# Graph attention and a routed FFN in one kernel: the first block's preparation moved ahead of a branch

## The chip, the cores and the metric

The kernel runs on one core of a Trainium2 chip. The core has a matrix engine (TensorE, PE, with its weight loads shown apart as PEld), a vector engine (VectorE, DVE), an activation engine (ScalarE, ACT), a general engine (GpSimd, POOL), a queue engine (SyncE, SP) and 16 DMA engines. [...] The metric is the device time of one execution in microseconds (us); lower is better.

## The reference

N = 4096 tokens of 256 numbers. A graph attention layer with four heads of 64 (mask `adj`, 4096 x 4096), a residual projection, ELU and layer norm; then a mixture of eight experts, two for each token. Cut to what matters here:

```
xn = layernorm(x)                                  # 4096 x 256
h = einsum('nd,hdk->hnk', xn, W)                   # 4 heads of 64
s_col = einsum('hnk,hk->hn', h, a1); s_row = einsum('hnk,hk->hn', h, a2)
e = leaky_relu(s_row[:, :, None] + s_col[:, None, :], 0.2)
att = softmax(where(adj > 0, e, -9e15), axis=-1)
out = einsum('hij,hjk->hik', att, h)
y = elu(out) + (xn @ Wr + br)
x = x + gamma * (y - mean(y)) / sqrt(var(y) + 1e-5) + beta
x = x + moe(layernorm(x))                          # top 2 of 8 experts, gelu
```

`adj` comes transposed; everything is float32, the masks bfloat16.

## The kernel before, in words

Tokens go in blocks of 512 (B; 8 blocks, NB) and row blocks of 128 (j, 32 of them, NT). Four sweeps (a, NR) each own 1024 rows of the output (R, two halves of 512), and run j over all 4096 columns.

*The attention of one j.* exp(leaky_relu(row + col)) is a product of factors: the larger of a row part (`er`, spread over all partitions) and a column part (`eb`), times a column factor that is multiplied into h (`ha`) and into the ones of the denominators (`unit`). So one DVE instruction for each head, `weigh` (L1067), makes w = max(er, eb) * mask, and PE adds up `acc` (L648, w times ha) and `den` (L657, w times unit). The mask `am` is loaded as int32 by SP and made bfloat16 by two ACT instructions (`load_mask`, L1055, L1056). w has ten buffers, the mask and its load three each.

*What must come first.* `norm_block(b)` (L520) loads 512 tokens (L523), takes mean and variance (`moments`, L173, L174), the root (`rstd_of`, with a square root on ACT, L138), normalises (xn, L528), transposes on PE (L533) and copies to `xT` on ACT (L537). `project_block(b)` (L542) makes h and the scores in one product (ph, L554, with `wall`: W and the score weights beside it) and the residual (pr, L578), subtracts a bound of the scores, `limit`, from the column scores and adds it to the row scores (sc, L561, L564), makes ed = exp of the column scores (L568) and ha (L569), the residual with its bias (rb, L583), and the row factor `part` (L593, L594), which is transposed (pp), copied (sp) and stored to `parts` in DRAM (L602). `load_rows` (L607) reads it back, the same numbers to all partitions, as `er`. Three PSUM banks (`bank`) serve pt, ph, pr, pp and pb in turn.

*The branch.* If `limit` is too large for the factors (`flag`), a general path is taken that works with maxima; with these inputs it is not. The branch (L976, L981) comes after `norm_block(0)`, `norm_block(1)`, `turn_biases` and the score weights (L469 to L497). Each engine reads the flag for itself. Behind it, in the path taken: `project_block(0)`, `load_rows`, then the sweep a = 0. Block b + 2 is normalised at j = 4b, and block b + 1 projected. Row blocks 0 to 3 are attended first for half 0 alone; then block 1 is projected, its row parts are loaded, and they are attended for half 1. From j = 4 on w has its full width of 1024.

The order inside an engine is a scheduler's, from dependences and priorities in program order; `issue_after(x)` makes it place what follows behind x, and `queue` fixes PE's order of acc and den. After sweep 0 nothing changes but the queue that an er is loaded on and its buffer.

Of the kernel before, what the change touches and what calls it, by code (L numbers as in the profile page):

```python
# [17 lines left out]
P = 128  # L18
# [22 lines left out]
def gat_then_moe(  # L41
# [49 lines left out]
    make_identity(nc, ident)  # L91

# [6 lines left out]
    nc.scalar.dma_start(wg[:, :, :E], Wg.rearrange("(c p) e -> p c e", p=P))  # L99
    bgb = const.tile([P, E], F32)  # L100
    nc.scalar.dma_start(bgb, over_partitions(bg, E))

    def numbers(name, shape, pattern, base=0, step=0):
        t = const.tile(shape, F32, name=name)
        nc.gpsimd.iota(
            t, pattern=pattern, base=base, channel_multiplier=step,
            allow_small_or_imprecise_dtypes=True,
        )
        return t
# [8 lines left out]
    nc.vector.tensor_scalar(before, ahead, 0.0, None, op0=OP.is_gt)  # L118
# [7 lines left out]
    nc.vector.tensor_copy(token16, token[:, :2])  # L126
# [21 lines left out]
    def mean_rstd(src):  # L148

        mv = moments(src)  # L150
        return mv, rstd_of(mv[:, :, 1], TB)

    def root_of(var, n):

        v = small.tile([P, n], F32, tag="v", name="v")
        nc.vector.tensor_scalar(v, var, EPS, None, op0=OP.add)
# [9 lines left out]
        return r  # L166
# [59 lines left out]
    nc.gpsimd.dma_start(b1r, b1.rearrange("e (c p) -> (e c) p", p=P))  # L226
# [222 lines left out]
    with ExitStack() as layer:  # L449
# [7 lines left out]
        ab = ab.rearrange("p (s k) -> p s k", s=2)  # L457
        for c in range(DC):
            nc.scalar.dma_start(
                wall[:, c, :HK].rearrange("p (h k) -> p h k", h=H),  # L460
                W[:, ts(c, P), :].rearrange("h p k -> p h k"),
            )
        nc.scalar.dma_start(ab[:, 0], over_partitions(a1, HK))
        nc.scalar.dma_start(ab[:, 1], over_partitions(a2, HK))
        nc.scalar.dma_start(wr, Wr.rearrange("(c p) d -> p c d", p=P))
        nc.scalar.dma_start(brm, over_partitions(br, D))
        nc.scalar.dma_start(gam, over_partitions(gamma, D))
        nc.scalar.dma_start(bet, over_partitions(beta, D))
        for c in range(DC):  # L469
            pr = large("wa").rearrange("p t d -> p (t d)")[:, : 2 * HK]  # L470
            pr = pr.rearrange("p (s k) -> p s k", s=2)
            nc.vector.tensor_tensor(
                pr, wall[:, c : c + 1, :HK].to_broadcast([P, 2, HK]), ab, OP.mult
            )
            nc.vector.tensor_reduce(
                wall[:, c, HK:], pr.rearrange("p s (h k) -> p (s h) k", h=H), AX.X, OP.add
            )

        nc.vector.tensor_scalar(brm, brm, -1.0, None, op0=OP.add)


        sq = gat.tile([P, H], F32)
        nc.vector.tensor_tensor(sq, wall[:, 0, HK : HK + H], wall[:, 0, HK : HK + H], OP.mult)
        for c in range(1, DC):
            s2 = gat.tile([P, H], F32, name=f"s2{c}")
            nc.vector.tensor_tensor(
                s2, wall[:, c, HK : HK + H], wall[:, c, HK : HK + H], OP.mult
            )
            nc.vector.tensor_tensor(sq, sq, s2, OP.add)
        long = gat.tile([P, H], F32)  # L490
        nc.gpsimd.partition_all_reduce(long, sq, P, bass_isa.ReduceOp.add)
        limit = gat.tile([P, H], F32)
        nc.scalar.activation(limit, long, AF.Sqrt, scale=1.01 * D)
        wide = gat.tile([P, 1], F32)
        nc.vector.tensor_reduce(wide, limit, AX.X, OP.max)
        flag = gat.tile([P, 1], I32)
        nc.vector.tensor_scalar(flag, wide, 0.5 * SPREAD, None, op0=OP.is_gt)  # L497

# [21 lines left out]
        def norm_block(b):  # L520

            xb = loaded("xb")
            nc.sync.dma_start(xb, rows_of(x, b))  # L523
            mv, r = mean_rstd(xb)
            pt = [bank([P, B], f"pt{c}") for c in range(DC)]
            for t in range(TB):
                xn = fin.tile([P, D], F32, tag="xn", name="xn", bufs=2)
                nc.vector.tensor_scalar(  # L528
                    xn, xb[:, t, :], mv[:, t, 0:1], r[:, t : t + 1],
                    op0=OP.subtract, op1=OP.mult,  # L530
                )
# [10 lines left out]
        def project_block(b, apart):  # L542
# [52 lines left out]
            else:  # L595
                nc.vector.tensor_copy(eb[:, here, :], cols)
                nc.vector.tensor_copy(turn, rows)
            pp = bank([H * TB, P], "pp")
# [3 lines left out]
            nc.gpsimd.dma_start(  # L602
                parts[:, ts(b, B)].rearrange("h (t p) -> h t p", p=P),
                sp,
            )

        def load_rows(er, b, n):  # L607

            src = parts[:, b * B : (b + n) * B]
            nc.scalar.dma_start(  # L610
# [301 lines left out]
        def last_block(b, u, z, given):  # L912
# [30 lines left out]
            r = root_of(mv[:, :, 1], TB)  # L943
# [7 lines left out]
            r = root_of(mv[:, :, 1], TB)  # L951
# [20 lines left out]

        norm_block(0)
        norm_block(1)
        turn_biases()
# [5 lines left out]
        with tc.If(general > 0) as chosen:  # L981

            with tc.tile_pool(name="gen", bufs=2) as work:
# [8 lines left out]
                for b in range(NB):  # L992
                    mine = range(b * B, (b + 1) * B)
                    rows = work.tile(full, F32, tag="er", name="er", bufs=1)
                    load_rows(rows, b, 1)
                    top = work.tile(full, F32, tag="top", name="top", bufs=1)
                    nc.vector.memset(top, -BIG)
                    for j in range(NT):
                        if j % TB == 0:
                            at = load_adj(work, mine, j, TB, 2)  # L1000
                        off = work.tile([P, B], F32, tag="off", name="off")
                        nc.vector.tensor_scalar(
                            off, at[:, j % TB, :], 0.0, -BIG, op0=OP.is_le, op1=OP.mult
# [12 lines left out]
                    for j in range(NT):  # L1016
                        if j % TB == 0:
                            at = load_adj(work, mine, j, TB, 2)
                        off = work.tile([P, B], F32, tag="off", name="off")
                        nc.vector.tensor_scalar(  # L1020
                            off, at[:, j % TB, :], 0.0, -BIG, op0=OP.is_le, op1=OP.mult
# [16 lines left out]
                    if b % HB == HB - 1 and b + 1 < NB:  # L1038
                        for _ in finish_blocks(b // HB):
                            pass  # L1040
# [292 lines left out]
```

## Time and profile before

| what | us |
|---|---|
| median of 3 runs | 1368.03 |
| lowest and highest of them | 1365.36, 1369.53 |
| the profiled execution | 1365.72 |
| its span, first to last instruction | 1364.0 |
| PE busy (matmuls) | 1292.6 |
| DVE busy | 868.1 |
| ACT busy | 597.2 |
| POOL busy | 226.6 |
| mean granted PE clock | 0.992 |

The profile is of one execution. A page lists groups of instructions with their busy time, the mean of one, and what ended the idle time ahead of them; the chain of waits goes back from the last instruction to what released it at each step; a timeline lists instructions in order of time; a view by stretches gives each engine's busy time in a stretch. The time is mostly three stages: preparation and sweep 0 to about 290 us, sweeps 1 to 3 to about 850, the experts after that. An idle engine costs time only where the engine that bounds the stage waits for it.

### The profile page before, as it was taken

What the parts mean: (1) busy time and instruction counts of PE and PEld (TensorE: products, weight loads), DVE (VectorE), ACT (ScalarE), POOL (GpSimd) and SP (SyncE); (2) the same over time, 40 slices, a digit from 0 to 9 for tenths busy, and PEclk for the clock granted to TensorE, in tenths of its full rate; (3) what the DMA queues carried; (4) which work ended last, traced back from release to release, by engine and by line L of the source; (5) the groups of instructions that cost most, each with busy time, mean ns of one, the idle gap of its engine ahead of it and who ended that gap; (6) DMA issues with size and microseconds to landing.
All of it is one profiled execution on the core that took longest, in us unless ns stands there. A gap on an engine that the chain in (4) does not pass through costs nothing.

```text
span 1364.0 us, 19028 instructions
## 1 busy us (share of the span) xinstructions
PE 1292.6 (95%) x7049; PEld 682.9 (50%) x7049; DVE 868.1 (64%) x1782; ACT 597.2 (44%) x1059; POOL 226.6 (17%) x189
## 2 busy tenths in 40 slices
PE   2889999999999999999999999999999999999996
PEld 1433333322222222222222222887788877888885
DVE  4789977878999989899999998665111111111110
ACT  1743533345566366654566552542333332333231
POOL 1000000000030300214000211125322212122221
PEclk9899999999999999999999999999999999999998
DMA  4654343343445444453333431977765665767671
GB/s 118 195 159 154 126 108 93 109 147 100 124 124 136 151 131 124 119 144 124 96 107 105 127 109 56 348 232 233 238 185 161 190 188 135 206 174 203 192 199 24
DMA packets 110270, 204.49 MB, mean 150 GB/s; under 512 B 8992, under 2 KB 77600, under 8 KB 110160
## 3 DMA queue, kind: packets, MB, share of 16 engines
q1 hardware_dynamic: 85792, 161.24, 37.7%
q0 software_dynamic: 19264, 32.27, 10.7%
q10 hardware_dynamic: 5104, 9.58, 2.4%
q8 instruction: 60, 0.98, 0.3%
q14 instruction: 50, 0.41, 0.1%
HBM read 173.99 MB, written 29.08 MB: 149 GB/s over the span
## 4 chain that ended last, share of the span: by engine, by line
PE 71%; DVE 19%; issue 3%; DMA 3%; ACT 2%; another core or an unknown queue 0%; ACTq 0%; POOL 0%; DVEq 0%; SPq 0%; POOLq 0%
PE acc L648 21%; PE po L1227 17%; PE ph L1207 16%; DVE w L1067 14%; PE den L657 10%; PE pr L578 1%; PE ph L554 1%; DMA b2b<-in_L_ffn_b 1%; DMA er<-parts 1%; PE pt L1189 1%; DVE y L874 1%; PE ptx L689 1%; DVE y L868 1%; PE pt L533 1%; DVE y L860 1%
## 5 line engine op out<-in xcount | busy, mean ns | idle before, releaser
L1067 DVE SCALAR_TENSOR_TENSOR w<-er,eb,am 128x1024 f32<-128x1024 f32 (+1 forms) x528 | 634.2, 1245 | 58.3 <-PE den L657 49.9
L648 PE MATMUL acc<-w,ha 128*64 128x512 f32 x2048 | 467.1, 601 | 7.2 <-DVE w L1067 5.0
L648 PEld LDWEIGHTS acc<-w,ha 128*64 128x64 f32 x2048 | 137.4, 137 | 301.7 <-issue 280.1
L1055 ACT ACTIVATE am<-adj 128x1024 bf16<-128x1024 int32 x132 | 139.5, 1057 | 287.8 <-DVE w L1067 280.2
L657 PE MATMUL den<-w,unit 128*2 128x512 f32 x2048 | 240.9, 593 | 7.7 <-DVE w L1067 6.7
L1207 PE MATMUL ph<-xT,w 128*128 128x256 f32 (+1 forms) x1056 | 241.9, 386 | 4.5 <-issue 2.4
L1227 PE MATMUL po<-w,hT 128*128 128x256 f32 x1088 | 240.6, 379 | 2.8 <-ACT hT L1211 2.8
L1211 ACT ACTIVATE hT<-ph,bias 128x256 f32<-128x256 f32 (+1 forms) x264 | 122.6, 476 | 257.2 <-PE ph L1207 252.8
L1207 PEld LDWEIGHTS ph<-xT,w 128*128 128x128 f32 x1056 | 199.9, 190 | 40.4 <-issue 3.2
L1227 PEld LDWEIGHTS po<-w,hT 128*128 128x128 f32 x1088 | 204.1, 190 | 29.6 <-ACT hT L1211 3.2
L1234 POOL DMA_INDIRECT out<-o,ids x68 | 107.0, 1574 | 357.5 <-DVE o L1231 188.3
L1231 DVE SCALAR_TENSOR_TENSOR o<-po,share,b2s 128x256 f32<-128x256 f32 x68 | 32.7, 482 | 192.3 <-PE po L1227 182.0
L1056 ACT ACTIVATE am<-am 128x1024 bf16<-128x1024 bf16 x132 | 139.3, 1057 | 2.9
L657 PEld LDWEIGHTS den<-w,unit 128*2 128x2 f32 x2048 | 44.7, 84 | 178.7 <-issue 152.0
L801 POOL DMA_INDIRECT lists<-xe,at x64 | 85.0, 1327 | 242.6 <-issue 127.3
L1193 DVE COPY xT<-pt 128x256 f32<-128x256 f32 (+1 forms) x29 | 12.6, 433 | 167.1 <-PE pt L1189 125.5
L1222 ACT ACTIVATE b2s<-b2b,share 128x256 f32<-128x256 f32 x68 | 31.5, 501 | 50.5 <-DMA b2b<-in_L_ffn_b 32.3
L878 POOL DMA_DIRECT2D out<-y x6 | 4.8, 800 | 256.0 <-DVE y L874 169.1
L554 PE MATMUL ph<-wall,xT 128*128 128x264 f32 x128 | 37.6, 418 | 7.7 <-DVE on L749 6.6
L578 PE MATMUL pr<-wr,xT 128*128 128x256 f32 x128 | 35.3, 403 | 2.6 <-ACT unit L568 0.9
L533 PE MATMUL pt<-ident,xn 128*128 128x128 f32 x64 | 14.7, 345 | 19.4 <-DVE xn L528 19.1
L554 PEld LDWEIGHTS ph<-wall,xT 128*128 128x128 f32 x128 | 25.3, 207 | 14.2 <-issue 8.1
(287 smaller groups left out, 640.6 us busy)
## 6 DMA issues: line engine op xcount, KB each, us to landing
adj<-in_adj SPq DMA_DIRECT2D x132, 512.0 KB
w<-in_L_ffn_W SPq DMA_DIRECT2D x66, 1024.0 KB
er<-parts ACTq DMA_DIRECT2D x3, 2048.0 KB
b2b<-in_L_ffn_b SPq DMA_DIRECT2D x33, 128.0 KB
early<-lists SPq DMA_DIRECT2D x16, 260.0 KB
xb<-in_x SPq DMA_DIRECT2D x8, 512.0 KB
residual<-rb POOLq DMA_DIRECT2D x8, 512.0 KB
rb<-residual SPq DMA_DIRECT2D x8, 512.0 KB
```

What stands on the lines that cost most here:

```text
L554: nc.tensor.matmul(ph, xT[:, c, ts(t, P)], wall[:, c, :], start=(c == 0), stop=(c == DC - 1),)
L578: nc.tensor.matmul(pr[:, t % 2, :], xT[:, c, ts(t, P)], wr[:, c, :], start=(c == 0), stop=(c == DC - 1),)
L648: queue(nc.tensor.matmul(acc[half][h // 2][ts(h % 2, K), :], ha[:, j, ts(h, K)], w[half][h], start=(j == 0), stop=(j == NT - 1),))
L657: queue(nc.tensor.matmul(den[h * Q : h * Q + HB, :], unit[:, j, h, 1 - half : 1 - half + HB], w[half][h], start=(j == 0 and half == 0), st ...
L801: ins = nc.gpsimd.indirect_dma_start(lists, bass.IndirectOffsetOnAxis(ap=at[:, k, t : t + 1], axis=0), xe[:, t, :], None,).ins
L1055: nc.scalar.activation(am, at[:, 0], AF.Relu)
L1056: nc.scalar.activation(am, am, AF.Sign)
L1067: nc.vector.scalar_tensor_tensor(wh[:, here], er[:, h, here], eb[:, j, h : h + 1], am[:, here], op0=OP.max, op1=OP.mult,)
L1207: order_of(nc.tensor.matmul(ph, job["w1"][:, c, ts(f, P)], xT[:, c, :], start=(c == 0), stop=(c == DC - 1),))
L1211: nc.scalar.activation(hT[:, f, :], ph, AF.Gelu, bias=job["bias"][:, f : f + 1])
L1227: order_of(nc.tensor.matmul(po, hT[:, f, ts(k, CH)], w2[:, f, :], start=(f == 0), stop=(f == FC - 1)))
L1234: nc.gpsimd.indirect_dma_start(job["into"], bass.IndirectOffsetOnAxis(ap=ids[:, k : k + 1], axis=0), o, None, compute_op=OP.add,)
```

## The change

- The root no longer uses ACT's square root in `norm_block` and for `limit`: `root_of` makes it with a first guess from the bits and three Newton steps on DVE. The sum over partitions for `limit` goes from POOL to two matmuls.
- Block 0 is loaded as four tiles; its normalisation is done by ACT instead of DVE.
- `project_first` projects block 0 ahead of the branch into the four acc banks, without the residual; `residual_first` makes that behind the branch. Block 0's row parts are stored on ACT's queue and loaded on SP's, ahead of the branch. The first two masks are made ahead of it too.
- The loads of a1 and a2 lead ACT's queue; five small ones go to POOL. POOL makes the identity before its counting tiles. `turn_biases` goes behind the branch. An Exp at the start loads ACT's table.
- Block 1's row parts are stored on ACT's queue instead of POOL's and loaded on SP's instead of ACT's.
- The general path (not taken) works in smaller tiles, so that er0 has room.

```diff
@@ -145,15 +149,11 @@
         nc.vector.tensor_tensor(r, r, q, OP.mult)
         return r
...
-    def root_of(var, n):
+    def root_of(var, n, part=1.0):
         v = small.tile([P, n], F32, tag="v", name="v")
-        nc.vector.tensor_scalar(v, var, EPS, None, op0=OP.add)
+        nc.vector.tensor_scalar(v, var, part, EPS, op0=OP.mult, op1=OP.add)
         r = small.tile([P, n], F32, tag="r", name="r")
         nc.vector.tensor_scalar(
             r.bitcast(I32), v.bitcast(I32), -0.5, 1597463007.0, op0=OP.mult, op1=OP.add
@@ -163,7 +163,7 @@
...
-        return r
+        return r, v
     def moments(src):
@@ -455,47 +454,54 @@
         brm = gat.tile([P, D], F32)
         ab = large("ab").rearrange("p t d -> p (t d)")[:, : 2 * HK]
         ab = ab.rearrange("p (s k) -> p s k", s=2)
+        nc.scalar.dma_start(ab[:, 0], over_partitions(a1, HK))
+        nc.scalar.dma_start(ab[:, 1], over_partitions(a2, HK))
         for c in range(DC):
             nc.scalar.dma_start(
                 wall[:, c, :HK].rearrange("p (h k) -> p h k", h=H),
                 W[:, ts(c, P), :].rearrange("h p k -> p h k"),
             )
-        nc.scalar.dma_start(ab[:, 0], over_partitions(a1, HK))
-        nc.scalar.dma_start(ab[:, 1], over_partitions(a2, HK))
         nc.scalar.dma_start(wr, Wr.rearrange("(c p) d -> p c d", p=P))
         nc.scalar.dma_start(brm, over_partitions(br, D))
-        nc.scalar.dma_start(gam, over_partitions(gamma, D))
-        nc.scalar.dma_start(bet, over_partitions(beta, D))
...
-        nc.vector.tensor_scalar(brm, brm, -1.0, None, op0=OP.add)
-        sq = gat.tile([P, H], F32)
-        nc.vector.tensor_tensor(sq, wall[:, 0, HK : HK + H], wall[:, 0, HK : HK + H], OP.mult)
...
-        long = gat.tile([P, H], F32)
-        nc.gpsimd.partition_all_reduce(long, sq, P, bass_isa.ReduceOp.add)
+        def rest_of_loads():
+            nc.gpsimd.dma_start(wg[:, :, :E], Wg.rearrange("(c p) e -> p c e", p=P))
+            nc.gpsimd.dma_start(bgb, over_partitions(bg, E))
+            nc.gpsimd.dma_start(gam, over_partitions(gamma, D))
+            nc.gpsimd.dma_start(bet, over_partitions(beta, D))
+            nc.gpsimd.dma_start(b1r, b1.rearrange("e (c p) -> (e c) p", p=P))
+        all1f = gat.tile([P, P], F32)
+        nc.vector.memset(all1f, 1.0)
         limit = gat.tile([P, H], F32)
-        nc.scalar.activation(limit, long, AF.Sqrt, scale=1.01 * D)
-        wide = gat.tile([P, 1], F32)
-        nc.vector.tensor_reduce(wide, limit, AX.X, OP.max)
         flag = gat.tile([P, 1], I32)
-        nc.vector.tensor_scalar(flag, wide, 0.5 * SPREAD, None, op0=OP.is_gt)
+        def scores_weights():
+            for c in range(DC):
...
+            sq = gat.tile([P, DC, H], F32)
+            nc.vector.tensor_tensor(sq, wall[:, :, HK : HK + H], wall[:, :, HK : HK + H], OP.mult)
+            pl = bank([P, H], "plim")
+            for c in range(DC):
+                nc.tensor.matmul(pl, all1f, sq[:, c, :], start=(c == 0), stop=(c == DC - 1))
+            r, v = root_of(pl, H, 1.01 * D)
+            nc.vector.tensor_tensor(limit, v, r, OP.mult)
+            wide = gat.tile([P, 1], F32)
+            nc.vector.tensor_reduce(wide, limit, AX.X, OP.max)
+            nc.vector.tensor_scalar(flag, wide, 0.5 * SPREAD, None, op0=OP.is_gt)
+        er0 = gat.tile([P, H, R], F32)
         ha = gat.tile([P, NT, HK], F32)
@@ -520,15 +526,31 @@
         def norm_block(b):
             xb = loaded("xb")
-            nc.sync.dma_start(xb, rows_of(x, b))
-            mv, r = mean_rstd(xb)
+            if b == 0:
+                for t in range(TB):
+                    nc.sync.dma_start(xb[:, t, :], x[ts(t, P), :])
+            else:
+                nc.sync.dma_start(xb, rows_of(x, b))
+            mv = moments(xb)
+            r, _ = root_of(mv[:, :, 1], TB)
+            if b == 0:
+                off = sums_of("off")
+                step.append(nc.vector.scalar_tensor_tensor(
+                    off, mv[:, :, 0], -1.0, r, op0=OP.mult, op1=OP.mult
+                ).ins)
             pt = [bank([P, B], f"pt{c}") for c in range(DC)]
             for t in range(TB):
                 xn = fin.tile([P, D], F32, tag="xn", name="xn", bufs=2)
-                nc.vector.tensor_scalar(
-                    xn, xb[:, t, :], mv[:, t, 0:1], r[:, t : t + 1],
-                    op0=OP.subtract, op1=OP.mult,
-                )
+                if b == 0:
+                    nc.scalar.activation(
+                        xn, xb[:, t, :], AF.Identity, bias=off[:, t : t + 1],
+                        scale=r[:, t : t + 1],
+                    )
+                else:
+                    nc.vector.tensor_scalar(
+                        xn, xb[:, t, :], mv[:, t, 0:1], r[:, t : t + 1],
+                        op0=OP.subtract, op1=OP.mult,
+                    )
                 for c in range(DC):
                     nc.tensor.transpose(pt[c][:, ts(t, P)], xn[:, ts(c, P)], ident)
             xT = (first_large if b < 2 else large)("xT")
@@ -595,19 +617,71 @@
             else:
                 nc.vector.tensor_copy(eb[:, here, :], cols)
                 nc.vector.tensor_copy(turn, rows)
+            store_parts(b, part, nc.scalar if b == 1 else nc.gpsimd)
+        def project_first():
+            sc = small.tile([P, TB, 2 * H], F32, tag="sc", name="sc")
+            cols, rows = sc[:, :, :H], sc[:, :, H:]
+            phs = [acc[t // 2][t % 2][:, : HK + 2 * H] for t in range(TB)]
+            for t in range(TB):
+                for c in range(DC):
+                    nc.tensor.matmul(
+                        phs[t], turned[0][:, c, ts(t, P)], wall[:, c, :],
+                        start=(c == 0), stop=(c == DC - 1),
+                    )
+                nc.vector.tensor_tensor(rows[:, t], phs[t][:, HK + H :], limit, OP.add)
+                nc.vector.tensor_tensor(
+                    cols[:, t], phs[t][:, HK : HK + H], limit, OP.subtract
+                )
+            part = small.tile([P, H, TB], F32, tag="part", name="part")
+            nc.vector.tensor_scalar(
+                part.rearrange("p h t -> p t h"), rows, 0.0, None, op0=OP.max
+            )
+            nc.scalar.activation(part, part, AF.Exp, scale=SLOPE - 1.0)
+            stored = store_parts(0, part, nc.scalar)
+            ed = unit[:, :TB, :, 1]
+            nc.scalar.activation(ed, cols, AF.Exp, scale=SLOPE)
+            nc.scalar.activation(eb[:, :TB, :], cols, AF.Exp, scale=1.0 - SLOPE)
+            step.append(stored)
+            for t in range(TB):
+                ins = nc.vector.tensor_tensor(
+                    ha[:, t, :].rearrange("p (h k) -> p h k", h=H),
+                    phs[t][:, :HK].rearrange("p (h k) -> p h k", h=H),
+                    ed[:, t].unsqueeze(2).to_broadcast([P, H, K]), OP.mult,
+                ).ins
+            step.append(ins)
+        def residual_first():
+            rb = residuals("rb")
+            for t in range(0, TB, 2):
+                pr = bank([P, 2, D], "pr")
+                for k in range(2):
+                    for c in range(DC):
+                        nc.tensor.matmul(
+                            pr[:, k, :], turned[0][:, c, ts(t + k, P)], wr[:, c, :],
+                            start=(c == 0), stop=(c == DC - 1),
+                        )
+                nc.vector.tensor_tensor(
+                    rb[:, t : t + 2, :], pr, brm.unsqueeze(1).to_broadcast([P, 2, D]), OP.add
+                )
+            nc.gpsimd.dma_start(rows_of(residual, 0), rb)
+        def store_parts(b, part, queue_of):
             pp = bank([H * TB, P], "pp")
             nc.tensor.transpose(pp, part.rearrange("p h t -> p (h t)"), ident)
             sp = small.tile([H * TB, P], F32, tag="sp", name="sp")
             nc.scalar.copy(sp, pp)
-            nc.gpsimd.dma_start(
+            return queue_of.dma_start(
                 parts[:, ts(b, B)].rearrange("h (t p) -> h t p", p=P),
                 sp,
-            )
-        def load_rows(er, b, n):
+            ).ins
+        def load_rows(er, b, n, queue_of):
             src = parts[:, b * B : (b + n) * B]
-            nc.scalar.dma_start(
+            queue_of.dma_start(
                 er,
                 bass.AP(
                     tensor=src.tensor, offset=src.offset, ap=[[0, P], [N, H], [1, n * B]]
@@ -970,9 +1044,32 @@
             last[0] = None
             listed.clear()
+        def load_mask(a, j):
+            at = load_adj(gat, range(a * R, (a + 1) * R), j, 1, 3)
+            am = gat.tile([P, R], BF16, tag="am", name="am", bufs=3)
+            nc.scalar.activation(am, at[:, 0], AF.Relu)
+            nc.scalar.activation(am, am, AF.Sign)
+            return am
+        warm = gat.tile([P, 1], F32)
+        nc.scalar.activation(warm, tiny, AF.Exp)
+        step = []
         norm_block(0)
-        norm_block(1)
-        turn_biases()
+        with tc.issue_after(step[-1]):
+            scores_weights()
+        project_first()
+        with tc.issue_after(step[-1]):
+            norm_block(1)
+            made_of_numbers()
+            nc.vector.tensor_scalar(brm, brm, -1.0, None, op0=OP.add)
+        with tc.issue_after(step[-2]):
+            first_masks = [load_mask(0, j) for j in range(2)]
+        load_rows(er0[:, :, :B], 0, 1, nc.sync)
+        rest_of_loads()
         general = nc.values_load(
             flag[0:1, 0:1], min_val=0, max_val=1,
             skip_runtime_bounds_check_because="a comparison gives 0 or 1",
@@ -1047,17 +1144,6 @@
             with tc.tile_pool(name="sep", bufs=2) as work:
...
                 def weigh(er, am, j, halves):
                     here = slice(halves[0] * B, (halves[-1] + 1) * B)
@@ -1073,9 +1159,10 @@
                     return w
                 both = list(range(HB))
-                project_block(0, True)
-                er = rows_parts()
-                load_rows(er[:, :, :B], 0, 1)
+                residual_first()
+                turn_biases()
+                ers = [er0, work.tile([P, H, R], F32, tag="er", name="er", bufs=1)]
+                er = er0
                 pending = None
                 for a in range(NR):
                     later = None
@@ -1084,10 +1171,11 @@
                             norm_block(j // TB + 2)
                         if a == 0 and j < TB:
-                            attend(weigh(er, load_mask(a, j), j, [0]), j, [0])
+                            am = first_masks[j] if j < len(first_masks) else load_mask(a, j)
+                            attend(weigh(er, am, j, [0]), j, [0])
                             if j == TB - 1:
                                 project_block(1, True)
-                                load_rows(er[:, :, B:], 1, 1)
+                                load_rows(er[:, :, B:], 1, 1, nc.sync)
                                 for i in range(TB):
                                     attend(weigh(er, load_mask(a, i), i, [1]), i, [1])
                             continue
@@ -1101,8 +1189,8 @@
                         if a + 1 == NR and j == 29:
                             first_tile()
                         if j == 20 and a + 1 < NR:
-                            later = rows_parts()
-                            load_rows(later, (a + 1) * HB, HB)
+                            later = ers[(a + 1) % 2]
+                            load_rows(later, (a + 1) * HB, HB, nc.scalar)
                     if a == 0:
                         mean_of_h()
                     er = later
```

The counting tiles get `issue_after` of the last instruction of the identity; `made_of_numbers` holds the two DVE conversions of `ahead` and `token` (L118, L126), and `mean_of_h`, `finish_blocks` and what follows them are as before.

## The prediction

> **What bounds the kernel now.** I read the page first: its span, its engine rows, its chain.
>
> ```profile
> span 1364.0 us, 19028 instructions
> PE   2889999999999999999999999999999999999996
> PE 71%; DVE 19%; issue 3%; DMA 3%; ACT 2%; another core or an unknown queue 0%; ACTq 0%; POOL 0%; DVEq 0%; SPq 0%; POOLq 0%
> L1067 DVE SCALAR_TENSOR_TENSOR w<-er,eb,am 128x1024 f32<-128x1024 f32 (+1 forms) x528 | 634.2, 1245 | 58.3 <-PE den L657 49.9
> ```
>
> TensorE (PE) is full in nearly every slice but the first (a slice is 34 us), and VectorE (DVE) waits for it, not it for DVE. The change touches only the start, so next come the stretches of the start (columns: busy us and instructions of PE, weight loads, DVE, ACT, POOL; granted clock; DMA):
>
> ```profile
> 27.00:66.00 39.00, 32.69 (x133) 18.35 (x135) 25.81 (x88) 25.00 (x37) 1.87 (x3) 0.91 0.66 204
> 66.00:80.00 14.00, 10.54 (x49) 6.97 (x45) 7.56 (x32) 5.52 (x15) 1.12 (x2) 1.00 0.62 189
> 80.00:92.00 12.00, 10.44 (x56) 2.22 (x56) 12.00 (x21) 7.75 (x8) 0.43 (x1) 0.86 0.42 129
> 92.00:118.00 26.00, 26.00 (x157) 7.93 (x151) 26.00 (x28) 12.26 (x17) 0.95 (x2) 1.00 0.45 144
> ```
>
> From 92 us PE has no gap. So whatever shortens the way there is gained whole, if PE then has as much work behind it. What lies on that way is in the chain of waits (start, us, what):
>
> ```profile
> 5.05 5.56 DMA ab<-in_L_gnn_a
> ...
> 18.63 1.32 PE pt L533 x4
> ...
> 23.66 3.67 issue
> ...
> 30.93 2.08 PE pr L578 x4
> ...
> 45.08 8.56 DMA er<-parts
> ...
> 72.05 7.77 DMA er<-parts
> ...
> 82.64 1.98 PE acc L648 x4
> ```
>
> Two loads of er (row parts of block 0, then of block 1, spread over all partitions) hold up the first attention; 3.67 us is the branch, and matmuls begin cold. Last, the timeline: where block 1's part is made, and where PE waits for DVE later.
>
> ```profile
> 65.34 0.17 DVE L593 TENSOR_SCALAR part<-sc 128x16 f32<-128x16 f32 x1
> ...
> 113.77 3.65 PE L648 MATMUL acc<-w,ha 128*64 128x512 f32 x16
> ...
> 148.19 0.44 PE L533 MATMUL pt<-ident,xn 128*128 128x128 f32 x2 [0.89 <-DVE xn L528]
> 179.57 0.44 PE L533 MATMUL pt<-ident,xn 128*128 128x128 f32 x2 [0.88 <-DVE xn L528]
> 210.84 0.44 PE L533 MATMUL pt<-ident,xn 128*128 128x128 f32 x2 [0.88 <-DVE xn L528]
> ```
>
> [...] flag written at 22.92, first DVE instruction of the taken side at 27.32, of PE at 27.95, of SP at 27.80; so 4.4 to 5.0 us, per engine, from its last instruction ahead of the branch. [...] four records of L578 take 2.08 us at 30.93 and 0.86 in a full stretch.
>
> **The change, part by part.** Times are of the profiled execution.
>
> (a) Up to block 0's xT. The x loads of block 0 become four and lead SP; ab leads ACT's queue, and five small loads go to POOL, behind its iotas, where nobody waits for them before the branch. The square root, its table load and its two hops to ACT go; root_of is 11 small DVE operations, each dependent on the last, at 0.2 us (L140 to L145 start at 16.30, 16.50, 16.70, 16.89). With the last x tile at 6.3 us (first statistics before: 6.34) DVE has the statistics at 6.9 and the offset, 12 operations on, at 9.3. ACT now does the four xn (0.5 each, from L1222's mean). But the identity is complete only at 11.66 (POOL, 11.38 + 0.28), as before; so PE starts at 11.7 instead of 16.2, and at 0.7 us per cold tile, with two xn buffers, ends at 14.9; xT at 16.0 (before 19.6). DVE's score weights (1.47 + 2 x 0.67) fit beside; the limit follows two tiny matmuls and 12 small operations by 16.5, under cover of the next step. The all-reduce on POOL and the ACT root go at no gain.
>
> (b) Block 0's projection ahead of the branch: eight matmuls[...]: done at 22. Part, exp, transpose, copy: 2 us; store issued at 24 and landed about 2.2 later (before: 2.5, 3.5 and 1.8 from issue of the store to that of the load), er issued at 26.2 on SP ahead of SP's branch, 7.8 us for the load: row parts at 34.
>
> (c) DVE ahead of the branch: four ha (1.4), block 1's statistics (1.8), three conversions (0.8), root (2.4), four xn with a wait for PE's cold transposes (2.4): from 22.7 to 31.8. The branch comes 8.9 us later than before, DVE's first w at 36.2 (before 53.66), PE's first instruction at 37.6. er at 34 is not what ends last.
>
> (d) After the branch. In the changed kernel's instruction order DVE has six w first, then residual_first's rb, then the norms of blocks 2 and 3 with the other ten half-width w, then block 1's projection. Counted up to block 1's part: 16 w x 0.67, 12 statistics x 0.35, 12 aggregates x 0.1, 6 xn x 0.35, 3 ha x 0.34, 3 rb x 0.6, some 50 small: 26 us. (The same prices on the old order from 27.3 to 65.4 give 25; the trace has 25.2.) residual_first runs cold on PE in front of the first attention: 2.1 + 2.1 + 1.9 + 1.0, so its two rb make DVE wait 1.7 and 1.2; waits for block 1's ph and pr I put at 0.9. So block 1's part comes at 36.2 + 26 + 3.8 = 66.0. Before it came at 65.34. The 17 us by which the first w is earlier are gone, because work that stood before the first w then stands behind it now.
>
> (e) From that part on: no table load and no POOL queue in the way; exp, transpose and copy 0.9, store 2.2, er with an x load ahead of it in SP's ring 8.3: 77.4 (before 79.85). Gain so far 2.4.
>
> (f) To the point where PE has no gap. DVE then has 16 half-width w and 8.9 us of other work (97.0), then sixteen full w at 1.2 with 11 us between: 127.2. PE ends row block 7 some 5.4 us on, at 132.6; before at 117.4. But in its order it has by then 14 ph, 16 pr and 12 transposes more behind it: 14 x 0.445 + 16 x 0.43 + 12 x 0.185 + 0.2 = 15.5. So 117.1 against 117.4: a gain of 0.3.
>
> (g) Later. Norm work being done early, DVE has 3.6 us besides w for the next four row blocks where it had 6 to 9, so the waits shown at 148, 179 and 210 should go: 2.65. Table loads of ACT in this stretch (1.28 each) go at nothing: ACT is busy 47% of the 26 us from 92. root_of costs DVE about 1 us a block, inside its slack. Rest unchanged.
>
> Sum: 0.3 + 2.65, about 3 us off an execution of 1365.7. The median of the runs is 1368.0; the same off it gives 1365.
>
> **Unknown costs.** Waits of DVE in (d): 3.8 taken; none would be 0, and between 27.3 and 65.4 DVE idled 38.1 - 25.2 = 12.9. er in (e): 7.8 if the SP ring is empty, 10 if it shares with adj and x loads. The clock in (b) and (d): all warm saves 4, all cold costs 3. Branch: 4.4 as before; a later flag gives no reason for less. ha and transposes waiting on ACT's four mask operations (1.06 each, ahead of block 1's xT): 0 to 2.
>
> **The rivals.** *The early start pays.* If DVE waits for nobody in (d), the store takes 1.8 and the ring is empty, another 3.8 + 0.4 + 0.5 come, and 2 if PE warms early: 1358. For it: er's first load at 34 and idle DMA between 12 and 28 us. Against: cold PE in front of the attention. *DVE's order decides (slower).* Up to row block 7 each wait of DVE goes through one to one. If it idles as it did, 12.9 instead of 3.8, the sum is 3 - 9: 1374. It decides from where block 1's part is later than 69 us, and makes the kernel measurably slower beyond 73. For it: DVE and PE feed each other there by sc, exp, ha and three PSUM banks. Against: those hops stand between other DVE work now. *It doesn't do what it says*: er lands late because store and load share rings with x and adj loads, at 42 instead of 34; 6 us of wait, 1371.
>
> **How the numbers follow.** What a measurement here can tell from no change is about 0.3%, 4.1 us. Forecast (1365, own range 1361 to 1369) 0.55; early start pays 0.22; DVE's order 0.18; late er 0.05. Of the forecast two fifths are below 1364, so faster 0.22 + 0.22 = 0.44; same 0.32 + 0.02 = 0.34; slower 0.18 + 0.03 + 0.01 = 0.22. The range 1357 to 1374 takes in both rivals' centres.
>
> **What would show it.** Right: first transpose of block 0 at about 12 us, store at 24, first w at 36 and ended by the branch, not by er; block 1's part at 64 to 68; second er at 75 to 80; no wait of PE for xn after 130. Wrong: first w ended by er beyond 40; the part before 61 or after 70; PE with gaps beyond 135; a different time in stages after 300 us, where nothing was changed.

## The result, and the profile after

| | us, median | lowest, highest |
|---|---|---|
| before | 1367.63 | 1365.36, 1369.53 |
| after | 1566.55 | 1563.21, 1569.53 |

The ratio is 1.1455, with a 95% interval of 1.1425 to 1.1484: the change makes the kernel 199 us slower. One run of five_masks, a kernel of the experiments, took 2258.62 us at a granted clock of 0.558, where its other eleven had 0.982 to 0.990, and is left out of its median and ratio. The page of after: its span, how busy PE was in forty equal slices and the clock granted to it there (in tenths, 9 is 90% or more), and three groups of instructions (busy us, mean ns of one, idle us ahead of them and what ended it):

```profile
span 1567.9 us, 19068 instructions
PE   3899998778888778887887787879999999999997
PEclk8999999989999989999999999999999999999998
L1153 DVE SCALAR_TENSOR_TENSOR w<-er,eb,am 128x1024 f32<-128x1024 f32 (+1 forms) x528 | 627.0, 1247 | 196.8 <-ACT am L1052 190.4
L722 PE MATMUL acc<-w,ha 128*64 128x512 f32 x2048 | 492.6, 623 | 53.1 <-DVE w L1153 52.9
L731 PE MATMUL den<-w,unit 128*2 128x512 f32 x2048 | 268.4, 644 | 102.7 <-DVE w L1153 102.6
```

The slices of the preparation are as good as before. The loss lies where no line of the attention itself was edited: from the seventh slice (235 us) to the 27th, the end of the sweeps, PE is at 7 or 8 tenths. The direction of waiting has turned round. Before, DVE's w waited 58.3 us in all, 49.9 of them for PE's den; now w waits 190.4 us for the mask (`am`), and PE waits for w. The number of w instructions and their mean length are the same. One stretch inside sweeps 1 and 2, the same 300 us of the clock before and then after (columns: busy us and instructions of PE, weight loads, DVE, ACT, POOL; granted clock, DMA share, GB/s):

```profile
300.00:600.00 300.00, 291.35 (x1792) 82.15 (x1786) 281.48 (x428) 171.18 (x286) 43.34 (x32) 1.00 0.44 127
```

```profile
300.00:600.00 300.00, 237.74 (x1316) 61.15 (x1312) 213.03 (x302) 126.21 (x207) 28.49 (x20) 0.92 0.34 100
```

No engine is full after the change; PE, the busiest, works 237.74 of 300 us. That fits a ring, engines that wait for each other in turn, and the timelines show one. First after (start and length in us), then before at the same place:

```profile
428.13 3.67 DVE L1153 SCALAR_TENSOR_TENSOR w<-er,eb,am 128x1024 f32<-128x1024 f32 x3
431.88 1.06 ACT L1051 ACTIVATE am<-adj 128x1024 bf16<-128x1024 int32 x1 [5.45 <-issue]
432.96 1.06 ACT L1052 ACTIVATE am<-am 128x1024 bf16<-128x1024 bf16 x1
434.06 4.87 DVE L1153 SCALAR_TENSOR_TENSOR w<-er,eb,am 128x1024 f32<-128x1024 f32 x4 [0.84 <-ACT am L1052]
439.01 1.06 ACT L1051 ACTIVATE am<-adj 128x1024 bf16<-128x1024 int32 x1 [2.09 <-issue]
```

```profile
434.49 1.27 DVE L1067 SCALAR_TENSOR_TENSOR w<-er,eb,am 128x1024 f32<-128x1024 f32 x1
434.51 1.06 ACT L1055 ACTIVATE am<-adj 128x1024 bf16<-128x1024 int32 x1 [1.94 <-DVE w L1067]
435.60 1.06 ACT L1056 ACTIVATE am<-am 128x1024 bf16<-128x1024 bf16 x1
435.79 1.28 DVE L1067 SCALAR_TENSOR_TENSOR w<-er,eb,am 128x1024 f32<-128x1024 f32 x1
439.68 1.06 ACT L1055 ACTIVATE am<-adj 128x1024 bf16<-128x1024 int32 x1 [3.02 <-DVE w L1067]
```

After: four w end, only then the Relu of the next mask starts, then its Sign, then the next four w. From Relu to Relu it is 439.01 - 431.88 = 7.13 us: 4.87 of w, 2.12 of ACT, 0.14 of hand-overs, for one j (a column block, as the expectations below call it). PE needs 5.3 us for one j: in the profile of before it does acc and den of two from 162.99 to 173.56 us. The view puts the waits of these two Relus down to "issue", that is to nothing that it could see; what they wait for comes next. Before: Relu and Sign run beside the w, for a later mask, and Relu follows Relu after 5.17 us. The kernel asks for three mask buffers both before and after, but after behaves as if it had one.

The built programs say why. The memory addresses that the 132 masks were given, and how many masks each address got:

```
before   44  44  44
after     1   1  130
```

Two addresses went to the two masks made ahead of the branch and were never given again; 130 masks share the third. In the program of after each Relu of the sweeps accordingly waits for the Sign of the mask just before it as well as for DVE; in that of before it waits for DVE alone.

### The profile page after: what moved, and what is told of

Read it like the earlier page. It is cut to its first block, busy times and chain, and to the rows that moved or that the text cites. A ratio compares the mean times of both kernels' runs of the same rounds, so it can differ in the third digit from the quotient of the medians.

```text
span 1567.9 us, 19068 instructions
## 1 busy us (share of the span) xinstructions
PE 1353.6 (86%) x7053; PEld 683.9 (44%) x7053; DVE 894.9 (57%) x1830; ACT 580.2 (37%) x1039; POOL 225.0 (14%) x190
## 5 line engine op out<-in xcount | busy, mean ns | idle before, releaser
L1153 DVE SCALAR_TENSOR_TENSOR w<-er,eb,am 128x1024 f32<-128x1024 f32 (+1 forms) x528 | 627.0, 1247 | 196.8 <-ACT am L1052 190.4
L722 PE MATMUL acc<-w,ha 128*64 128x512 f32 x2048 | 492.6, 623 | 53.1 <-DVE w L1153 52.9
L731 PE MATMUL den<-w,unit 128*2 128x512 f32 x2048 | 268.4, 644 | 102.7 <-DVE w L1153 102.6
L731 PEld LDWEIGHTS den<-w,unit 128*2 128x2 f32 x2048 | 41.4, 86 | 288.8 <-issue 145.3
L576 PE MATMUL ph<-wall,xT 128*128 128x264 f32 x112 | 33.3, 416 | 5.0 <-DVE rb L605 5.0
L921 ACT ACTIVATE y<-ptr,z 128x64 f32<-128x64 f32 x96 | 21.9, 324 | 34.5 <-PE ptr L919 30.5
L600 PE MATMUL pr<-wr,xT 128*128 128x256 f32 x112 | 30.6, 391 | 1.1 <-ACT xT L559 1.1
L609 POOL DMA_DIRECT2D residual<-rb x7 | 5.5, 779 | 157.1 <-DVE rb L605 97.6
```

What stands on the lines that cost most here:

```text
L576: nc.tensor.matmul(ph, xT[:, c, ts(t, P)], wall[:, c, :], start=(c == 0), stop=(c == DC - 1),)
L722: queue(nc.tensor.matmul(acc[half][h // 2][ts(h % 2, K), :], ha[:, j, ts(h, K)], w[half][h], start=(j == 0), stop=(j == NT - 1),))
L731: queue(nc.tensor.matmul(den[h * Q : h * Q + HB, :], unit[:, j, h, 1 - half : 1 - half + HB], w[half][h], start=(j == 0 and half == 0), st ...
L1153: nc.vector.scalar_tensor_tensor(wh[:, here], er[:, h, here], eb[:, j, h : h + 1], am[:, here], op0=OP.max, op1=OP.mult,)
```

## The experiments

The theory: *held buffers*. A mask that is allocated ahead of the branch keeps its buffer until the branch is over. Rivals: the *pool* (`load_mask` now takes its tiles from a pool opened ahead of the branch), and the *row parts* (one buffer of er ahead of the branch and one behind, other queues). In the table, "given" counts the buffers that the kernel asks for under the masks' name `am`, "held" those that masks made ahead of the branch keep, and "free" those left for the masks of the sweeps. Each ratio is to the kernel before as it ran beside that kernel; its medians there were 1364.85 to 1367.63 us, so kernels that ran apart are compared by ratio.

| kernel | given, held, free | us | ratio to before | 95% interval |
|---|---|---|---|---|
| after | 3, 2, 1 | 1566.55 | 1.1455 | 1.1425 to 1.1484 |
| masks_inside | 3, 0, 3 | 1366.02 | 1.0007 | 0.9995 to 1.0019 |
| masks_in_er0 | 3, 0, 3 | 1362.59 | 0.9994 | 0.9984 to 1.0004 |
| before_one_mask | 1, 0, 1 | 1566.70 | 1.1480 | 1.1454 to 1.1505 |
| before_two_masks | 2, 0, 2 | 1360.30 | 0.9973 | 0.9961 to 0.9986 |
| one_early_mask | 3, 1, 2 | 1359.59 | 0.9941 | 0.9919 to 0.9963 |
| five_masks | 5, 2, 3 | 1369.88 | 1.0025 | 1.0014 to 1.0037 |
| one_step_mask | 3, 2, 1 | 1430.78 | 1.0465 | 1.0438 to 1.0491 |
| own_masks | 2, 0, 2 | 1359.17 | 0.9936 | 0.9919 to 0.9953 |
| masks_in_er0_two | 2, 0, 2 | 1361.12 | 0.9951 | 0.9934 to 0.9968 |
| four_xn | 2, 0, 2 | 1358.28 | 0.9932 | 0.9915 to 0.9949 |
| late_residual | 2, 0, 2 | 1360.90 | 0.9954 | 0.9940 to 0.9968 |
| own_mask_four_xn | 2, 0, 2 | 1356.54 | 0.9924 | 0.9911 to 0.9938 |

**What costs the 199 us.** The line that makes the first masks is moved behind the branch:

```diff
-        with tc.issue_after(step[-2]):
-            first_masks = [load_mask(0, j) for j in range(2)]
...
+                first_masks = [load_mask(0, j) for j in range(2)]
                 residual_first()
```

> The changed kernel with its first two masks made inside the branch instead of ahead of it; same pool, same tag, same three buffers, same addresses. Theory of the held buffers (the two masks made ahead of the branch keep two of the three buffers until the branch is over, so that 130 masks share one): 1360 to 1372 us, the relu of the next mask beside the w of this one. Rival, the pool (a mask in the pool opened ahead of the branch waits too strictly, wherever it is made): 1555 to 1575. Rival, the row parts' second buffer or its queue: 1555 to 1575 too.

1366.02: the whole loss is gone, with the same pool, three addresses of 44 masks each, and the row parts as the change has them. Pool and row parts fall. Next, the masks stay early but lie elsewhere:

```diff
...
-            first_masks = [load_mask(0, j) for j in range(2)]
+            first_masks = [load_mask(0, j, er0[:, j, B:].bitcast(BF16)) for j in range(2)]
```

> The changed kernel with its first two masks still made ahead of the branch, but written into the half of er0 that is empty until the second row block, so that none of the three mask buffers is held. Held buffers: 1357 to 1370 us, and if the early masks are worth anything, up to 5 us below the kernel with the masks made inside. Rival, that a mask made ahead of the branch itself is what holds the sweeps up: 1555 to 1575. Rival, the pool or the row parts' buffer: 1555 to 1575.

1362.59: making masks early is not what hurts, holding their buffers is. The two loads of `adj` are still made ahead of the branch here, so their buffers are not it either. Then the loss put into the kernel before, by `bufs=1` in place of 3 for `am`, and the step between, `bufs=2`:

> The kernel before with one mask buffer instead of three and nothing else changed. Held buffers: the whole loss comes with it, 1555 to 1580 us, with the relu waiting for the fourth w of each column block. Rivals (pool, row parts): little of the loss, 1365 to 1420.

> The kernel before with two mask buffers instead of three. Held buffers: with two, relu and sign of the next mask (2.1 us) run beside the four w (4.9 us), so most of the loss is gone: 1365 to 1385 us. If the wait grows in step with the number of buffers taken away: about 1465. Rivals: 1365 to 1370.

One buffer gives 1566.70, a ratio of 1.1480 where after has 1.1455, the same within their intervals. Its group of w answers to that of after:

```profile
L1067 DVE SCALAR_TENSOR_TENSOR w<-er,eb,am 128x1024 f32<-128x1024 f32 (+1 forms) x528 | 626.8, 1247 | 192.5 <-ACT am L1056 189.9
```

The same 190 us of waiting for the mask. Two buffers lose nothing and are even 0.27% faster than three. So the price is a step between two and one, not a slope; one early mask (`range(1)`) says the same of the change itself:

> The changed kernel with one mask made ahead of the branch instead of two, nothing else. Held buffers: one of three is held, the sweeps have two, and with two the kernel before lost nothing, so 1357 to 1366 us. Rival, that any mask made ahead of the branch holds the sweeps up, or that the loss grows by the held buffer: 1450 to 1480.

1359.59, within its range: with one early mask in place of two the change is 0.59% faster than before, by an interval that excludes no change. And `bufs=5`, for which one of the ten w buffers was given up:

> The changed kernel with five mask buffers instead of three, so that three are left beside the two held ones; the memory comes from one of the ten w buffers. Held buffers: 1357 to 1368 us although both early masks and the pool are untouched. Rival, that the early masks' place or the pool matters and not the count: 1550 to 1570.

1369.88, 2 us beyond the range, but the 199 us are gone with both early masks in place. At PE's first wait for xn after 140 us this kernel was 3.7 us ahead of before (144.52 against 148.19), at the first expert 4.9 behind (859.0 against 854.1). The nine w buffers are the edit that reaches the sweeps; I didn't try them alone, so why it lost 8.6 us there is open. Last, the ring itself, by leaving the Relu out of it:

```diff
-            nc.scalar.activation(am, at[:, 0], AF.Relu)
-            nc.scalar.activation(am, am, AF.Sign)
+            nc.scalar.activation(am, at[:, 0], AF.Sign)
```

> The changed kernel with the mask made by one ACT instruction (Sign alone) instead of two; the Relu, which clamps negative entries, is left out. Theory of the ring: with one free buffer a column block takes four w (4.87 us), Relu and Sign (1.06 each) and their hand-overs one after another, 7.1 us; without Relu 6.05, so 132 masks x 1.08 = about 142 us less, 1420 to 1440 us, still slower than before because PE needs less than 6 us. Rival, that ACT's time is not in the ring (the next mask waits for something else, such as the load of adj): 1550 to 1570.

1430.78, 136 us less where 142 were worked out: the Relu stands in the ring nearly one to one (1.03 us a mask for its 1.06).

**What the change is worth without its fault.** Early masks in buffers of their own:

```diff
-            am = gat.tile([P, R], BF16, tag="am", name="am", bufs=3)
...
+            if first:
+                am = gat.tile([P, B], BF16, tag="am0", name="am0", bufs=2)
+            else:
+                am = gat.tile([P, R], BF16, tag="am", name="am", bufs=2)
...
```

> The changed kernel with the two early masks in buffers of their own, half as wide (only their first 512 columns are read), and two buffers for the masks of the sweeps: as much memory as three masks. Held buffers: the loss goes. Row parts not held up as in the kernel with the masks in er0 (there their load was issued at 27.4 us, behind the mask writes, against 24.8 in the changed kernel): first w at 34 to 35 us, and what was 2.7 us ahead of before at the norm of 145 us becomes 4 to 6. Time 1354 to 1361 us, ratio 0.993 to 0.998. Rival, that a start earlier by 2 us is taken back in the row blocks 0 to 2: the same as the next kernel, 1357 to 1363.

> The kernel with the early masks in er0, and two buffers in place of three for the masks of the sweeps. Two mask buffers gave the kernel before 0.27%: if that adds to the early masks' gain, 1354 to 1361 us (ratio 0.992 to 0.998). If both are the same 3 us (the ACT order in the first row blocks), 1359 to 1363 (0.997 to 1.000).

> The kernel with the early masks in er0 and two mask buffers, and four xn buffers in place of two. My step (g) had said that the three waits of PE for xn go because the norms have less company on DVE; they stayed at 0.71, 0.88 and 0.88 us. If they come from the two xn buffers (the third xn is queued behind w on DVE until PE has turned the first), they go with four: 2.5 us less than the kernel with two xn buffers, no wait of PE for xn over 0.35 us after 130 us. Rival, that xn stands behind w on DVE whatever its buffers: the waits stay, no difference.

1359.17 is within its range. 1361.12 is 0.1 us beyond one range and within the other, but its ratio, 0.9951 (to 0.9968), lies in that of the first case alone, which speaks for two gains that add. four_xn, 1358.28, is 2.8 us below it; the two ran side by side, and all six runs of four_xn (1357.57 to 1359.46) are below all six of masks_in_er0_two (1359.66 to 1361.55), so this difference is clear though their intervals against before overlap. The timeline shows the first waits of PE for xn in own_masks, and what stands in their place in four_xn (`bufs=4` for xn on top of masks_in_er0_two):

```profile
143.23 0.76 PE L555 MATMUL pt<-ident,xn 128*128 128x128 f32 x4 [0.63 <-DVE xn L550]
173.80 0.44 PE L555 MATMUL pt<-ident,xn 128*128 128x128 f32 x2 [0.88 <-DVE xn L550]
```

```profile
145.22 1.13 PE L600 MATMUL pr<-wr,xT 128*128 128x256 f32 x4 [0.62 <-ACT xT L559]
179.04 1.13 PE L576 MATMUL ph<-wall,xT 128*128 128x264 f32 x4 [0.87 <-DVE sc L586]
```

own_masks is 5.0 us ahead of before at the first (148.19) and 5.8 at the second (179.57). With four xn buffers the waits for xn are gone; a wait for xT or sc, about as long, comes instead, and yet by the first wait of sweep 1 the kernel is 2.2 us ahead of its like with two (287.07 against 289.27). Fewer waits are the smaller part of that: for the same matmuls from 140 us on (to 218.9 with two buffers, to 216.7 with four) PE waited 2.4 us and then 1.9, but its 24 transposes, eight at a stretch instead of four or two, were busy 3.3 us instead of 4.5, and the 158 acc 36.3 instead of 37.2. So the 2.5 us that were expected came, but mostly not as waits saved, and that part was luck.

Then residual_first, moved from the start of the branch to just ahead of block 1's projection in own_masks:

> The kernel with the early masks in buffers of their own, and residual_first moved from the start of the branch to just ahead of block 1's projection. Step (d) had put 2.9 us of DVE waiting on its cold matmuls in front of the first attention. If they are paid there, block 1's part, at 60.4 us in the kernel with own masks, comes at 57.5 to 59.5, and the time falls by 1 to 2 us. Rival, that its work is only moved behind the first attention and into the way of block 1's projection: part at 60 to 62, same time.

The time, 1360.90, can't be told from that of own_masks (the intervals overlap), but the stage differs: block 1's part came at 66.49 us instead of 60.38, later than the rival had allowed. At the start of the branch, in own_masks, these matmuls run from 34.56 to 40.62 us, where DVE makes its first six w (33.80 to 37.87); put later, they stand between those of the attention and of block 1 (49.35 to 59.7 us), ahead of block 1's projection. That this is what delays the part is read from the timeline, not tested. And the best parts together, with one early mask:

> One early mask in a buffer of its own and half as wide, two buffers for the masks of the sweeps, four xn buffers. If the gains of own masks (4 us by 180 us against masks in er0) and of four xn (2.2 us between 145 and 287 us) add up: 1353 to 1358 us, ratio 0.990 to 0.993. If not: 1357 to 1360.

1356.54, 0.76% faster than before, with an interval that excludes no change. It is the fastest of all; that the two gains add up in full isn't shown, as its interval overlaps those of own_masks and four_xn.

## Why the prediction was wrong

It was 1365, and 1566.55 was measured. The step that failed is (g), in two words: "Rest unchanged." In its place the sweeps' w waited 190.4 us for their masks. The cost of the early masks was put down only in the unknowns, as ACT time ahead of block 1's xT, 0 to 2 us. That they *own* two of three buffers for the length of the branch was priced nowhere, and no rival had it. The prediction's signs of being wrong did name "a different time in stages after 300 us, where nothing was changed". But something was: `load_mask` had moved, and the description before the prediction is wrong where it calls the er's queue and buffer the only change after sweep 0. A buffer count was read as a supply, when it is a limit on what is alive at once. The ring could have been priced from the page of before: four w at 1.25, two mask operations at 1.06, 7.1 us for one j, against the 5.3 that PE needs.

Of the other steps, in the profile of after up to where the masks bite:

```profile
21.88 0.18 DVE L638 TENSOR_SCALAR part<-sc 128x16 f32<-128x16 f32 x1
22.98 1.19 ACTq L676 DMA_DIRECT2D parts<-sp  x1
24.84 0.38 SPq L684 DMA_DIRECT2D er<-parts  x1
34.50 2.08 DVE L1153 SCALAR_TENSOR_TENSOR w<-er,eb,am 128x512 f32<-128x512 f32 x3 [4.65 <-DMA er<-parts]
61.90 0.18 DVE L615 TENSOR_SCALAR part<-sc 128x16 f32<-128x16 f32 x1
74.25 2.08 DVE L1153 SCALAR_TENSOR_TENSOR w<-er,eb,am 128x512 f32<-128x512 f32 x3 [1.79 <-DMA er<-parts]
```

- (a), (b): the times nearly right. The first transposes came at 10.95 (11.7 forecast), but not for the identity's sake: POOL had it done at 1.76 us, not at 11.66 as before, and PE waited for ACT's xn. ACT's table load at the early Exp took 1.28 us, at 6.24. Block 0's eight matmuls, whose end at 22 was an estimate, ran from 15.39 to 21.64. The part began at 21.88, the store issued at 22.98 (24) and the load at 24.84 (26.2). From the load's issue to the first w it was 9.7 us, not 7.8.
- (c): the time nearly right, 34.50 against 36.2, the reason wrong: DVE was done with block 1's xn at 29.85, not 31.8, and er ended last by the profile, though the branch (4.4 us before) was over at nearly the same time. In own_masks, where the load was issued at 24.2, er did not end last: w began at 33.80, 4.60 us after DVE's last instruction ahead of the branch.
- (d): 61.90 against 66.0. The start was 1.7 earlier; between the two DVE was busy 24.9 (26 forecast) and idle 2.5 (3.8). The matmuls of residual_first were slow (its 16 records on PE have a median of 631 ns, the 112 of the later blocks one of 379), but the two waits for them were 1.5 together, not 2.9, and late_residual shows that its place is cover rather than cost.
- (e): 74.25 against 77.4. The earlier part gave 4.1 us; the way from it took 12.4, not 11.4: from the load's issue, at 64.78 behind an x load at 64.34, to the first w it was 9.5 us, where the 8.3 of the forecast was an estimate.
- (f): 0.3 us was too little. With free buffers the change is 2.7 (masks_in_er0) or 5.0 (own_masks) ahead at 145 us. Most of that came from the earlier steps: at the second er own_masks was 6.7 ahead (73.17 against 79.85), where 2.4 were forecast, and on the way to 145 us it lost 1.7, where 2.1 were forecast. I had counted that way on the changed kernel's own order of instructions, in which w comes four at a time with everything else between (74.25, 79.21, 84.49 and 89.73 us): the order that held buffers make. In own_masks the order is before's kind again, and from the second er to block 3's part it takes 46.4 us (to 119.59), before 45.5 (to 125.30).
- (g): the three waits for xn were to go for lack of other norm work on DVE. They stayed in own_masks, at 0.63, 0.88 and 0.88 us, and went with four buffers, though others came in their place: with two, the third xn stands behind w on DVE until PE has turned the first (in before it began at 147.73 us, as four w begun at 142.94 ended).

So the 3 us of the sum were made of two errors, too little up to (f) and too much in (g). That masks_in_er0 is 2.7 us ahead at 145 us is therefore no proof of the sum; its time, 0.06% below before, can't be told from no change. Of the 0.64% of own_masks some 0.27% may be what two buffers give the kernel before as well.

Two of the prediction's readings of the branch before were off: SP's first instruction behind it is at 27.37 us, not 27.80, and the 5.0 us of PE run from the flag; from PE's last instruction ahead of the branch it was 6.59.

The loss adds up. The span grew by 203.9. PE was not busy for 214.3 us after and 71.4 before, 142.9 more; the other 61.0 are longer matmuls (1353.6 busy against 1292.6, with the same work), den 644 ns for 593, acc 623 for 601.

## What to carry to other kernels

Before moving an allocation ahead of a branch or loop, count what stays alive across it: a tile made outside and read inside took its buffer out of rotation, and the instructions that then wait are far from the edit. The built program shows it without a run, in the addresses given to the tiles of one name and in a wait of each producer for the one before. A stage with no full engine may be a ring: add up its members' durations once around (here 7.13 us), and compare that with what the bounding engine needs (5.3).

## What the runs showed of the hardware

PE was granted less than its full clock where its waits were short. In after the longest wait of PE between 300 and 420 us was 2.84 us, and in nine of the 24 stretches of 5 us there the granted clock was under full, 0.50 to 0.94; over 300 to 600 us it was 0.92, before 1.00. The wait of 2.84 us came after 13 us of matmuls without one, and half clock followed; after one of 2.51 us the clock stayed full (first lines from the timeline, second ones from the view by stretches: PE's busy us and instructions, granted clock, DMA share, GB/s):

```profile
334.63 1.97 PE L722 MATMUL acc<-w,ha 128*64 128x512 f32 x4 [2.84 <-DVE w L1153]
335.00:340.00 5.00, 4.58 (x12) 0.50 0.15 33
```

```profile
360.27 1.90 PE L731 MATMUL den<-w,unit 128*2 128x512 f32 x16 [2.51 <-DVE w L1153]
360.00:365.00 5.00, 4.73 (x30) 1.00 0.93 197
```

That the waits cost the clock, and how long one has to be for it, these runs don't show. The ends of matmuls are modelled in the profile, so the length of such a wait is not exact.

Two mask buffers in place of three took 0.9973 of before's time. With three mask buffers ACT's order had the Relu of a later mask ahead of the four u (which take acc out of PSUM at the end of sweep 0), and that Relu had to wait 1.87 us for a w; with two buffers the Relu came behind them. Before, then before_two_masks:

```profile
292.24 1.06 ACT L1055 ACTIVATE am<-adj 128x1024 bf16<-128x1024 int32 x1 [1.87 <-DVE w L1067]
293.21 2.40 ACT L816 ACTIVATE u<-acc,hbar 128x512 f32<-128x512 f32 x4
```

```profile
289.57 2.42 ACT L816 ACTIVATE u<-acc,hbar 128x512 f32<-128x512 f32 x4 [1.07 <-DVE hbar L629]
```

PE's wait for u fell from 2.22 to 0.47 us. That is 1.75 of the 3.6 us by which before_two_masks is ahead there (290.31 against 293.93); 1.9 it had by 177.71 (179.57), from a cause that I didn't trace.
